# A two-layer graph attention kernel: moving layer 1's softmaxes, its selection matrices and its key gathers

## The chip, the cores and the metric

The kernel runs on one core of a Trainium2 chip. The metric is the device time of one execution in microseconds. Before the change three runs took 2463.49, 2476.31 and 2496.46 us; the median, 2476.31 us, is the time to be compared.

## The reference

A graph of N = 3125 nodes with 768 features has 53125 edges (both directions of 25000, and one loop per node), sorted by destination, each of one of three relations. Two layers of relational graph attention follow each other, and a layer norm of the residual ends it. One layer is

```
xr = einsum('nd,rdf->rnf', x, W)            # every node, every relation
oi, oj = xr[etype, dst], xr[etype, src]
alpha = leaky_relu(oi @ q + oj @ k, 0.2)    # per edge and head
e = exp(alpha - segment_max(alpha, dst)[dst])
a = e / (segment_sum(e, dst)[dst] + 1e-16)
out = segment_sum(a * oj, dst) + b
```

with four heads of 192 features in layer 1 and one head of 768 in layer 2. Between the layers stands an elu; the result is `layernorm(x + layer2(elu(layer1(x))))`. All values are float32.

## The kernel before

The nodes are cut into NB = 25 blocks of 128 destinations. The edges of a block are held in slots of 128 edges: SL = 18 slots a block, SLL = 9 in the last and smaller one, NK = 441 in all. An edge is a partition, a slot a column.

Matrix products of nearly float32 accuracy are made of reduced-precision parts: an operand is split in a high part H and a remainder L, and three products (H·H, H·L, L·H) are summed. Where one operand is exact, as a 0/1 matrix is, two are enough.

The work has four stages, each emitted in an order written out by hand; each engine runs its own instructions in that order:

- **Preparation** (`prepare`, `weights_kq`, `nodes_kq`): edge lists are put into DRAM, and the weights are split into `wH` and `wL`, kept in SBUF. Each node's key and query values are computed for every relation: the keys go to the DRAM table `kt1`, the queries stay in SBUF and are split in three bf16 parts, `q1s`.
- **Layer 1's products and softmaxes** (`phase1`): 144 groups of 18 matmuls make `xr`, half a row (384 columns) of one block and relation each (`d_group`, L629). ScalarE copies a group from PSUM into one of three row buffers (`d_row`, L641), and every second group sends the row to the DRAM table `tab1` on SP's queue. Between the groups stand the steps of the softmaxes, one block for each six groups: `a_index` and `a_index2` turn the edge lists into gather indices `ridx` and local destinations `dl`; `a_gathers` fetches the keys of 18 slots from `kt1` with indirect DMAs that GpSimd issues (L451); `a_q`, `a_q2`, `a_q3` bring the queries to the edges; `a_alpha` (L565) adds keys and queries; `a_max` (three TensorE transposes, L573), `a_scan` (two VectorE scans, and ScalarE's Exp, L586), `a_back` (a transpose) and `a_put` give the weights `pall`. The list `steps` holds at which group each step of a block stands: its gathers five groups before the block's first group, `a_alpha` four after, `a_max` five after; block 24 has a list of its own, `last`. Three buffers `kt0` to `kt2` hold the keys. Layer 2's weights are split in the same stage, and x plus a bias is stored for the end (`w_load`, `w_split`, `d_split`).
- **Layer 1's sums and layer 2's products** (`phase2`): a loop over slots k. GpSimd gathers the 128 rows of slot k from `tab1` into one of the nine buffers `share` (L451). `high` makes H, the rows times the edge weights, on ScalarE, four instructions (L788), and `sel`, a 128 x 128 matrix that is 1 where an edge (partition) belongs to a destination (column), with one compare on VectorE for each third slot, on GpSimd for the others (L790). `low` makes the remainder L on VectorE (L802), and `sums` multiplies `sel` with H and L into PSUM, four matmuls (L821). Slot k is gathered in step k, reaches `high` in step k+5, `low` in k+6 and `sums` in k+8 (LAG = 8). A few of the first eight slots take another form (`whole`). When a block is complete, `e_y` to `e_s2` give the elu and its transposes (L833 to L864), and 108 matmuls (`d_part`, L876), six for each slot of the next block, make layer 2's rows for the table `tab2`. The blocks come in the order 24, 0, 1, ... 23.
- **Layer 2's sums** (`phase3`): the same for one head, with the softmaxes inside the loop, and the layer norm.

All work of `phase2` on `tab1` begins when its last row has been stored, since any edge may need any row.

Of the kernel before, what the change touches and what calls it, by code (L numbers as in the profile page):

```python
# [45 lines left out]
PART = 6  # L46

# [4 lines left out]
def kernel(  # L52
# [50 lines left out]
    w2_d = dram.tile([R * DT * P, 2 * D], F32, name="w2_d")  # L103

# [16 lines left out]
    q1s = keep.tile([P, NB, H1, R, 3], BF, name="q1s")  # L121
# [344 lines left out]

    def a_load(pre, b):
        s = a_st[b] = {}
        r0 = start(b, regs)
        s["T"] = pre.tile([3 * SL, P], F32, name="T", bufs=2)  # L470
        nc.sync.dma_start(s["T"], at(ed_d, 0, 0, [[LL, 3], [P, SL], [1, P]], r0))
# [26 lines left out]
    def phase1(pre, work, psum, wH, wL, qq):  # L498
        kts = [work.tile([P, SL, H1], F32, name=f"kt{i}", bufs=1) for i in range(3)]
# [3 lines left out]
        rows = share[:3]  # L503
# [4 lines left out]
        def a_window(b):  # L508
            s = st[b]
            s["f"] = work.tile([H1 * SL, 3 * P + 1], F32, name="w", bufs=2)  # L510
            nc.sync.dma_start(s["f"], at(ed_d, 3, -P - 1, [[P, SL], [0, H1], [1, 3 * P + 1]], start(b, regs)))
# [15 lines left out]

        def a_gather(b, j):
            gather_rows(kts[b % 3][:, j, :], kt1, b, j)
# [19 lines left out]
        def a_q3(b):  # L549
# [9 lines left out]
            s["qe"] = work.tile([P, SL, H1], F32, name="qe", bufs=2)  # L559
            V.tensor_reduce(s["qe"], tq, AX.X, ALU.add)  # L560

        def a_alpha(b):
            s = st[b]
            a = work.tile([P, SL, H1], F32, name="a", bufs=2)
            V.tensor_add(a, s["qe"], kts[b % 3])  # L565
            s["al"] = als[b % 2]
            V.scalar_tensor_tensor(s["al"][:, 1:SL + 1, :], a, NEG_SLOPE, a, op0=ALU.mult, op1=ALU.max)

        def a_max(b):
            s = st[b]  # L570
            pa = psum.tile([P, 512], F32, name="pa", bufs=1)
            for c in range(3):
                T.transpose(pa[:H1 * SL, c * P:(c + 1) * P],  # L573
                            s["al"].rearrange("p j h -> p (j h)")[:, c * H1:(c + SL) * H1], ident)
            s["pa"] = pa

        def a_scan(b):
            s = st[b]
            pa, f = s["pa"], s["f"]
            F, B = (share[i][:H1 * SL, b % 2 * HW:b % 2 * HW + n] for i, n in ((7, 3 * P), (8, 2 * P)))  # L580
            V.tensor_tensor_scan(F, f[:, 0:3 * P], pa[:H1 * SL, :3 * P], -3e38, op0=ALU.add, op1=ALU.max)
            V.tensor_tensor_scan(B[:, ::-1], f[:, P + 1:3 * P + 1][:, ::-1], F[:, P:3 * P][:, ::-1], -3e38,
                                 op0=ALU.add, op1=ALU.max)
            s["e"] = work.tile([H1 * SL, P], F32, name="e", bufs=2)
            V.tensor_sub(s["e"], pa[:H1 * SL, P:2 * P], B[:, :P])
            S.activation(s["e"], s["e"], AF.Exp)  # L586

        def a_back(b):
            s = st[b]
            pT = s["pT"] = psum.tile([P, 512], F32, name="pT", bufs=1)  # L590
            T.transpose(pT[:, :H1 * SL], s["e"], ident[:H1 * SL, :H1 * SL])

        def a_put(b):
            pT = st.pop(b)["pT"]
            V.tensor_copy(pall[:, b].rearrange("p j h -> p (j h)"), pT[:, :H1 * SL])
# [39 lines left out]
        def d_row(b, r, c):  # L635
# [3 lines left out]
            o = rows[len(n_rows) % 3]  # L639
# [28 lines left out]
        def slots(b):  # L668
            return SLL if b == NB - 1 else SL

        a_index(0)
        a_index2(0)
        for j in range(SL):
            a_gather(0, j)
        for b in range(2):
# [6 lines left out]

        def a_gathers(b):
            for j in range(slots(b)):
                a_gather(b, j)
# [7 lines left out]
        def x_next(b):  # L693
# [6 lines left out]
        ev = {}  # L700

        steps = ((-9, a_loads), (-9, a_loads2), (-6, a_index), (-5, a_index2), (-5, a_gathers), (1, a_q), (2, a_q2),
                 (2, a_window), (3, a_q3), (4, a_alpha), (5, a_max), (6, a_scan), (7, a_back), (8, a_put))
        last = ((-14, a_loads), (-9, a_loads2), (-9, a_index), (-8, a_index2), (-8, a_gathers), (-4, a_q), (-3, a_q2),
                (-3, a_window), (-2, a_q3), (-1, a_alpha), (0, a_max), (1, a_scan), (2, a_back), (3, a_put))
        for b in [*reversed(range(NB - 1)), NB - 1]:
            for d, f in steps if b < NB - 1 else last:

                d += 2 * (d >= 4 and b < 8)
                if 6 * b + d >= 0:  # L710
                    ev.setdefault(6 * b + d, []).append((f, b))
# [3 lines left out]
        for n in range(max(ev) + 1):  # L715
# [25 lines left out]
            if 0 < n <= len(groups):  # L741
                d_row(*groups[n - 1])


    def phase2(work, psum, wH, wL):
# [10 lines left out]
        blk = {}  # L756

        order = [NB - 1, *range(NB - 1)]
        ends2 = {SLL + i * SL - 1 for i in range(NB)}

        def slot(k):

            if k < SLL:
                return NB - 1, k
            return divmod(k - SLL, SL)
# [9 lines left out]
        def high(k):  # L775
# [13 lines left out]
            sel = work.tile([P, P], F32R, name="sel", bufs=4)  # L789
            (V if k % 3 == 0 else G).tensor_scalar(sel, row, dl[:, b, j:j + 1], None, op0=ALU.is_equal)  # L790
            st[k] = [sel, H]

        def low(k):
# [4 lines left out]
            H = st[k][1]  # L798
# [7 lines left out]
        def sums(k):  # L806
# [11 lines left out]
            sel, H, L = st.pop(k)  # L818
            for i, a in enumerate((H, L)):
                for c in range(2):  # L820
                    T.matmul(acc[:, c, :HW], sel, a[:, c * HW:(c + 1) * HW], start=(j == 0 and i == 0),  # L821
# [78 lines left out]

        LAG = 8
        first = SLL + LAG - 1
# [842 lines left out]
```

## Time and profile before

| | |
|---|---|
| median of the timed runs | 2476.31 us |
| the profiled execution's own time | 2296.29 us |
| its span | 2294.5 us |
| mean granted TensorE clock | 0.955 |
| TensorE, VectorE, ScalarE, GpSimd busy | 2047.2, 1685.4, 1172.9, 1749.5 us |
| first gather of keys | 123.2 us |
| first gather of `tab1`'s rows | 738.2 us |
| first and last elu (L839) | 763.3 and 1581.0 us |
| moved by DMA | 508.20 MB |

The profile was taken in one execution. TensorE is PE (PEld loads its stationary operand), VectorE DVE, ScalarE ACT, GpSimd POOL; SP is the engine that issues most plain DMAs. Matmuls are pipelined, so that one that follows another shows some 340 ns and costs 177. A wait is named by who waited and what ended it last. "issue" is time in which the engine waited for nothing that the profile shows. The profiled execution is shorter than any of the timed ones; the two are kept apart below.

### The profile page before, as it was taken

How to read it: one execution, taken by the hardware profiler on the slowest of the kernel's cores; microseconds unless marked ns; L12 is line 12 of the kernel's file. 1: busy time of each engine (PE TensorE's matmuls, PEld its weight loads, DVE VectorE, ACT ScalarE, POOL GpSimd, SP SyncE). 2: the span in 40 equal slices, each digit the busy share in tenths (PEclk: the TensorE clock that was granted, in tenths of full speed). 3: DMA queues.
4: the chain of work that ended last, by engine and by line, in shares of the span. 5: the costliest groups of instructions: out<-in, count | busy, mean ns of one | idle time of the engine just before them, and what ended most of it. 6: DMA issues, size and time to landing. Idle time of an engine off the chain costs nothing.

```text
span 2294.5 us, 37251 instructions
## 1 busy us (share of the span) xinstructions
PE 2047.2 (89%) x11055; PEld 1758.8 (77%) x11055; DVE 1685.4 (73%) x4377; ACT 1172.9 (51%) x2620; POOL 1749.5 (76%) x1685
## 2 busy tenths in 40 slices
PE   6998878998885899999999999999498898899886
PEld 5888878888885889999999999999255555555554
DVE  7734434434432899999999999995388888898887
ACT  5411111111111788888888888884144444444443
POOL 4267777777776888888888888883777777777773
PEclk9999999999998899999999999999699999999998
DMA  6554544444455977778777777775888888888882
GB/s 178 179 154 158 177 137 158 165 153 143 158 191 166 316 237 232 228 231 244 236 229 234 230 234 238 232 231 202 282 280 293 288 296 279 286 278 283 282 269 72
DMA packets 153593, 508.20 MB, mean 221 GB/s; under 512 B 40404, under 2 KB 53723, under 8 KB 153383
## 3 DMA queue, kind: packets, MB, share of 16 engines
q0 software_dynamic: 85472, 334.19, 48.1%
q1 hardware_dynamic: 57681, 155.56, 18.8%
q10 hardware_dynamic: 10230, 15.98, 2.2%
q8 instruction: 91, 1.49, 0.3%
q14 instruction: 119, 0.97, 0.1%
HBM read 428.40 MB, written 94.04 MB: 228 GB/s over the span
## 4 chain that ended last, share of the span: by engine, by line
PE 35%; DVE 14%; POOL 7%; issue 6%; DMA 5%; ACT 1%; POOLq 0%; DVEq 0%; ACTq 0%
PE po L876 15%; PE acc L821 11%; PE acc L1091 7%; DMA G<-ftab,ridx 4%; DVE L L1080 4%; POOL share L451 3%; POOL sel L790 2%; DVE selp L1062 1%; DVE L L802 1%; DVE sT L986 1%; POOL G L451 1%; DVE sel L1071 1%; DMA G<-ftab,rfirst 1%; PE pt L851 1%; DVE stats L1109 1%
## 5 line engine op out<-in xcount | busy, mean ns | idle before, releaser
L788 ACT ACTIVATE H<-share,pall 128x193 fp32r<-128x193 f32 x1748 | 644.0, 447 | 106.9 <-DMA share<-ftab,ridx 43.5
L802 DVE SCALAR_TENSOR_TENSOR L<-share,pall,H 128x193 fp32r<-128x193 f32 x1748 | 648.9, 437 | 28.6 <-ACT H L788 14.1
L876 PE MATMUL po<-wH,hT 128*128 128x386 f32 (+1 forms) x1800 | 533.2, 339 | 0.0
L451 POOL DMA_INDIRECT G<-ftab,ridx x378 | 432.5, 1144 | 115.2 <-issue 54.0
L451 POOL DMA_INDIRECT kt<-kt,ridx x378 | 405.7, 1073 | 115.2 <-issue 114.6
L451 POOL DMA_INDIRECT share<-ftab,ridx x378 | 428.6, 1134 | 81.4 <-DVE L L802 42.6
L629 PE MATMUL po<-wH,xT 128*128 128x384 f32 x1584 | 445.2, 354 | 0.4 <-issue 0.2
L1091 PE MATMUL acc<-G,selp 128*128 128x386 f32 x904 | 355.5, 519 | 1.1 <-DVE selp L1062 1.1
L876 PEld LDWEIGHTS po<-wH,hT 128*128 128x128 f32 x1800 | 334.6, 189 | 0.6 <-DVE hT L864 0.5
L876 PE MATMUL po<-wL,hT 128*128 128x386 f32 (+1 forms) x900 | 304.9, 339 | 0.0
L629 PEld LDWEIGHTS po<-wH,xT 128*128 128x128 f32 x1584 | 302.1, 196 | 2.9 <-DVE xT L616 0.5
L629 PE MATMUL po<-wL,xT 128*128 128x384 f32 x792 | 275.4, 348 | 0.0
L821 PE MATMUL acc<-H,sel 128*128 128x386 f32 x874 | 241.9, 358 | 22.0 <-POOL sel L790 12.1
L641 ACT COPY share<-po 128x384 f32<-128x384 f32 x144 | 69.0, 479 | 339.4 <-PE po L629 274.4
L1091 PEld LDWEIGHTS acc<-G,selp 128*128 128x128 f32 x904 | 169.7, 199 | 89.1 <-issue 23.0
L790 POOL TENSOR_SCALAR sel<-frow,fdl 128x128 fp32r<-128x128 f32 x291 | 224.8, 773 | 13.4 <-PE acc L821 1.5
L821 PE MATMUL acc<-L,sel 128*128 128x386 f32 x874 | 226.5, 340 | 0.0
L1080 DVE SCALAR_TENSOR_TENSOR L<-G,p,H 128x772 fp32r<-128x772 f32 x215 | 217.5, 1013 | 1.4 <-issue 0.7
L1066 ACT ACTIVATE H<-G,p 128x772 fp32r<-128x772 f32 x215 | 189.8, 927 | 47.5 <-issue 34.0
L821 PEld LDWEIGHTS acc<-H,sel 128*128 128x128 f32 x874 | 149.8, 189 | 55.7 <-POOL sel L790 46.7
L565 DVE TENSOR_TENSOR a<-qe,kt 128x72 f32<-128x72 f32 x25 | 5.9, 238 | 242.3 <-DMA kt<-kt,ridx 205.3
L876 PEld LDWEIGHTS po<-wL,hT 128*128 128x128 f32 x900 | 169.7, 189 | 0.0
(229 smaller groups left out, 2902.8 us busy)
## 6 DMA issues: line engine op xcount, KB each, us to landing
ftab<-r SPq DMA_DIRECT2D x75, 386.0 KB
ftab<-share SPq DMA_DIRECT2D x72, 386.0 KB
sT<-dr_d SPq DMA_DIRECT2D x25, 576.0 KB
share<-in_L_gnn_W_dram SPq DMA_DIRECT2D x36, 384.0 KB
w_d<-w2hl SPq DMA_DIRECT2D x18, 768.0 KB
share<-in_x_dram SPq DMA_DIRECT2D x25, 384.0 KB
xb_d<-share SPq DMA_DIRECT2D x25, 384.0 KB
xr<-in_x_dram SPq DMA_DIRECT2D x23, 384.0 KB
```

The source lines that it names most:

```text
L451: G.indirect_dma_start(out=to, out_offset=None, in_=tab, in_offset=_index(i[:, j:j + 1]), bounds_check=NP * R - 1, oob_is_err=False)
L629: T.matmul(po[:, :HALF], xT[:, s, t, :], w[:, i, sl], start=(n == 0), stop=(n == 3 * DT - 1))
L641: S.copy(to, po[:, :HALF].rearrange("p (h f) -> p h f", h=2))
L788: S.activation(H[:, c], g[:, c], AF.Copy, scale=pall[:, b, j, h:h + 1])
L790: (V if k % 3 == 0 else G).tensor_scalar(sel, row, dl[:, b, j:j + 1], None, op0=ALU.is_equal)
L802: V.scalar_tensor_tensor(L[:, c], g[:, c], pall[:, b, j, h:h + 1], H[:, c].bitcast(F32), op0=ALU.mult, op1=ALU.subtract)
L821: T.matmul(acc[:, c, :HW], sel, a[:, c * HW:(c + 1) * HW], start=(j == 0 and i == 0), stop=(k in ends2 and i == 1), skip_group_check=True)
L851: T.transpose(pt[:, t // 3, (t % 3) * P:(t % 3 + 1) * P], s["ey"][:, t * P:(t + 1) * P], ident)
L876: T.matmul(po[:, :wd], hT[:, k, t, :], w[:, r * DT + t, sl], start=(t == 0 and n == 0), stop=(t == DT - 1 and n == 2))
L1066: S.activation(H, g, AF.Copy, scale=p)
L1080: V.scalar_tensor_tensor(L, g, blk[b]["p"][:, j:j + 1], st[k][1].bitcast(F32), op0=ALU.mult, op1=ALU.subtract)
L1091: T.matmul(acc[:, c, :HW], sel, a[:, c * HW:(c + 1) * HW], start=(j == 0 and i == 0), stop=(k in ends and i == len(parts) - 1))
```

## The change

- **The order and pace of the softmaxes.** `phase1` takes the blocks in the order of `phase2`: 24, 0, 1, ... 23. With i a block's place in it, gathers stand at group 6i-5, the queries at 7i+3 or earlier (at least five groups before those of the next block, and within the 144 groups), and `a_alpha` to `a_put` at 7i+6 to 7i+10, so one block for each seven groups.
- **The last five blocks** (SPILL = 5) get their queries in `phase1`, kept in `qlast`, which lies in the memory of `q1s` where that is no longer needed. Their softmaxes run in `phase2`'s loop (`c_window` to `c_put`), in the gap after a block's elu, with `y` and `ey` as scratch. For the last three (LATE = 3) the 54 key gathers are issued there too, one every five slots.
- **The keys** are gathered straight into `pall`, where the weights come later; `kt0` to `kt2` are gone. GpSimd clears `pall` at the start.
- **The selections** are made in `phase1` by ScalarE: Abs(dl - row) for each slot, and for six slots at once Relu(1 - that), in the buffer `share[6]`; SP stores the six in the new DRAM table `sel_d` (74 stores). In `phase2` SP loads them back, two slots at a time, into three buffers (221 loads), a load being asked for when `sums` has used a pair.
- **A fourth row buffer** in `phase1`.

The steps `a_alpha` to `a_put` keep their instructions; they are taken out of `phase1` so that both stages can use them.

```diff
+    G.memset(pall, 0.0)
...
+    def a_gather(b, j):
+        gather_rows(pall[:, b, j, :], kt1, b, j)
...
+        rows = [*share[:3], work.tile([P, RW], F32, name="row3", bufs=1)]
...
+            i = order1.index(b) - (NB - SPILL)
+            s["qe"] = qlast[i] if i >= 0 else work.tile([P, SL, H1], F32, name="qe", bufs=5)
...
+        def s_slot(k):
+            b, j = slot1(k)
+            S.activation(share[6][:, k % SC * P:(k % SC + 1) * P], row, AF.Abs, bias=dl[:, b, j:j + 1], scale=-1.0)
+        def s_store(c):
+            n = (min((c + 1) * SC, NK) - c * SC) * P
+            to = share[6][:, :n]
+            S.activation(to, to, AF.Relu, bias=1.0, scale=-1.0)
+            nc.sync.dma_start(sel_d[c * P:(c + 1) * P, :n], to)
...
-        for b in [*reversed(range(NB - 1)), NB - 1]:
-            for d, f in steps if b < NB - 1 else last:
+        for i, b in enumerate(order1):
+            when = []
+            q = min(7 * i + 3, NG - 1 - 5 * (NB - 1 - i))
+            if i > 1:
+                when += [(6 * i - 14, a_loads), (q - 8, a_loads2)]
+            if i > 0:
+                when += [(6 * i - 6, a_index), (6 * i - 5, a_index2)]
+                if i < NB - LATE:
+                    when += [(6 * i - 5, a_gathers)]
+            when += [(q, a_q), (q + 1, a_q2), (q + 2, a_q3)]
+            if i < NB - SPILL:
+                when += [(7 * i + d, f) for d, f in ((2, b_window), (6, b_alpha), (7, b_max), (8, b_scan), (9, b_back),
+                                                     (10, b_put))]
...
+        for k in range(NK):
+            i = order1.index(slot1(k)[0])
+            n = max(6 * i - 4, k // 3)
+            ev2.setdefault(n, []).append((s_slot, k))
+            if k % SC == SC - 1 or k == NK - 1:
+                ev2.setdefault(n, []).append((s_store, k // SC))
...
+        def s_load(c):
+            k = 2 * c
+            if k >= NK:
+                return
+            n = min(2, NK - k) * P
+            sels[c] = work.tile([P, 2, P], F32R, name="sel", bufs=3)
+            nc.sync.dma_start(sels[c].bitcast(F32).rearrange("p s n -> p (s n)")[:, :n],
+                              sel_d[k // SC * P:(k // SC + 1) * P, k % SC * P:k % SC * P + n])
...
-            sel = work.tile([P, P], F32R, name="sel", bufs=4)
-            (V if k % 3 == 0 else G).tensor_scalar(sel, row, dl[:, b, j:j + 1], None, op0=ALU.is_equal)
...
-                    T.matmul(acc[:, c, :HW], sel, a[:, c * HW:(c + 1) * HW], start=(j == 0 and i == 0),
+                    T.matmul(acc[:, c, :HW], sels[k // 2][:, k % 2], a[:, c * HW:(c + 1) * HW], start=(j == 0 and i == 0),
...
+        late = [(b, j) for b in order[NB - LATE:] for j in range(SL)]
+        for i, (b, j) in enumerate(late):
+            when(20 + 5 * i, a_gather, b, j)
+        for i, b in enumerate(order[NB - SPILL:]):
+            k = 20 + 5 * SL * max(i + 1 - (SPILL - LATE), 0) + 4
+            m = max(k - SLL - LAG, 0) // SL + 1 + (i if i < SPILL - LATE else 0)
+            k = SLL + m * SL + LAG + 6
+            for d, f in ((0, c_window), (4, c_alpha), (4, c_max), (5, c_scan), (6, c_back), (7, c_put)):
+                when(k + d, f, b)
...
             if 0 <= k - LAG < NK:
                 sums(k - LAG)
+                if (k - LAG) % 2:
+                    s_load((k - LAG) // 2 + 3)
```

## The prediction

> **What bounds the kernel now.** I read the page's slices first, then busy time by stage, then the waits of each stage, then the tiles on its critical wait.
>
> ```profile
> PE   6998878998885899999999999999498898899886
> ...
> POOL 4267777777776888888888888883777777777773
> PEclk9999999999998899999999999999699999999998
> ```
>
> Each digit is a 57 us slice. Three stages stand out, cut at the two dips. Busy time in each (engines in the order PE, PEld, DVE, ACT, POOL, then clock, DMA share, GB/s):
>
> ```profile
> 122.00:737.00 615.00, 532.51 (x3303) 510.63 (x3303) 241.49 (x521) 107.13 (x210) 471.55 (x441) 0.95 0.49 161
> ...
> 763.00:1581.00 818.00, 802.04 (x4430) 767.52 (x4431) 781.67 (x2272) 709.12 (x1911) 705.38 (x713) 1.00 0.77 236
> ...
> 1607.00:2294.00 687.00, 577.95 (x2439) 354.92 (x2439) 555.26 (x1273) 279.29 (x335) 514.43 (x453) 0.92 0.81 266
> ```
>
> The first is layer 1's products with its softmaxes (phase1), the second layer 1's sums with layer 2's products (phase2), the third layer 2's sums. In the first, TensorE is idle for 82 us and its clock is below full. The key gathers, from the tile's view, and the waits of the stage (in total, times, longest) say why:
>
> ```profile
> L451 POOL DMA_INDIRECT kt<-kt,ridx x378: 992/997/1769, 196.5 to 716.1; - x189
> L451 POOL DMA_INDIRECT kt<-kt,rfirst x63: 992/997/1582, 123.2 to 727.8; - x63
> ```
>
> ```profile
> DVE a L565 <- DMA kt<-kt,ridx: 205.3, 21, 15.1
> ...
> POOL kt L451 <- issue: 133.1, 437, 0.3
> PEld pa L573 <- DVE al L567: 73.0, 22, 9.0
> PE pa L573 <- DVE al L567: 66.1, 22, 8.7
> ```
>
> 441 gathers start from 123.2 to 727.8 us: 604.6/440 = 1.374 us each (997 ns and 0.30 of "issue"), with no other gap. GpSimd paces the stage; VectorE waits for the keys, and TensorE, in order, for VectorE at the transposes `pa`. One such stop, and the end of the stage:
>
> ```profile
> 420.53 0.86 PE L573 MATMUL pa<-fident,al 128*72 128x128 f32 x3 [2.42 <-DVE al L567]
> ...
> 421.83 0.84 PE L629 MATMUL po<-wH,xT 128*128 128x384 f32 x2
> ```
>
> ```profile
> 738.24 1.00 POOL L451 DMA_INDIRECT share<-ftab,rfirst  x1 [9.42 <-ACT e L586]
> ```
>
> After the 2.42 us stop a pair of matmuls takes 0.84 us where it took 0.52. At the end GpSimd idles 9.4 us while the last softmax and table row finish.
>
> In the second stage the waits name GpSimd again, but they are small:
>
> ```profile
> PEld acc L821 <- POOL sel L790: 46.7, 106, 2.4
> ```
>
> ```profile
> L790 POOL TENSOR_SCALAR sel<-frow,fdl 128x128 fp32r<-128x128 f32 x291 | 224.8, 773 | 13.4 <-PE acc L821 1.5
> ...
> L790 DVE TENSOR_SCALAR sel<-frow,fdl 128x128 fp32r<-128x128 f32 x146 | 45.8, 314 | 0.0
> ```
>
> GpSimd's 705 busy and 0.3 us of issue for some 430 gathers fill its 818 us; VectorE is at 96% and TensorE at 98%. Three engines are within a few per cent of the bound.
>
> **What the Trainium skill says.** "TensorE: Matmul & The Clock Gate", Part 1: after about an idle window of 3.4 us the array runs at half clock until it has been busy as long again. The trace agrees: 0.84 against 0.52 us above. So a wait removed here gives back more than itself. "GPSIMD Engine Reference", Specifications: its SBUF interface is shared with VectorE, with contention where a VectorE instruction has two SBUF inputs. L802 has two, and its durations run from 400 (median 409) to 687 ns, which fits but does not prove it. "ScalarE: Activation LUTs", Table sets: abs and relu are in every set, so Abs, Relu, Exp and Copy should need no table load; no run here shows it. "DMA: Bandwidth & Descriptors", Anatomy of one DMA: about 2 us fixed and little for 128 KB; the chain of waits has a 386 KB table store landing in 2.33 us.
>
> **The change part by part.**
>
> *Key gathers, first stage.* 54 of 441 (last three blocks) leave it. 387 x 1.374 = 532 us, from 123.2 to 655. The destination `pall` needs no buffer to come free; a block's gathers wait only for its index, made 6i-5 groups in, always earlier than GpSimd arrives.
>
> TensorE without stops: between two stops in the timeline 18 matmuls take 3.18 us, six groups with the transposes 21.2. 144 groups are 24 x 21.2 = 509 us, from 122 to about 631. (Check: 532 busy, less about 25 at half clock.) Softmax i now sits at group 7i+6, at 122+3+3.53(7i+6) = 146+24.7i; its last key is issued at 134+24.7i and is used 3.7 us later (727.83 to 731.56 in the timeline). Some 8 us to spare for every i: the stops go. GpSimd at 655 is then later than TensorE and its last table row (631 + 0.5 copy + 2.3 landing). Sums start at about 658 instead of 738.2: **-80 us**. The 9.4 us tail is in it.
>
> *Selections.* ScalarE gets 441 Abs of 128 columns with a pointer bias. The Trainium skill's price ("ScalarE: Activation LUTs", What ACT_TABLE_LOAD costs) is 280 + 0.833 x 128 = 387 ns, less 93 of overlap; L586, 72x128, took 310. I take 0.31: 137 us. Plus 74 Relu of 768 columns at 0.83 (as the cast L660): 61. ScalarE goes from 107 to 305 of 530 us. One staging tile, `share[6]`, must be stored before the next six are made: about 2.6 us, covered by the 3.5 us of a product group before ScalarE is due there again. Without that cover: 74 times the excess. The stores stand on SP ahead of table rows and loads. On GpSimd 225 us go, on VectorE 46.
>
> *Their loads.* 221 of 128 KB on SP, three buffers, each asked for when TensorE has done with a pair and needed four slots later: 5 x 1.77 - 0.7 = 8 us. At 2.3 to 5 us landing they cost nothing; above 8, everything behind them on TensorE stands.
>
> *Second stage.* Blocks pass at (1581.0-763.3)/24 = 34.07 us (first and last start of L839). Ten matmuls of a slot take 1.77 us undisturbed, six transposes 0.57: 18 x 1.77 + 0.57 = 32.4. At most 24 x 1.65 = 40 us. VectorE: 782 - 46 + 14 = 750 of 790, still under TensorE; GpSimd: 432 x 1.4 + 54 x 1.374 = 680, no longer full.
>
> *Five late softmaxes there.* Each: one window load, VectorE 0.24+0.23+0.94+0.69+0.29+0.22 = 2.6 us, one exp of 0.31, four transposes, some 0.7 us of TensorE. In front of c_max TensorE waits for c_alpha, which is queued behind a slot's L; sums and products are queued behind that. Bounds: nothing to 4 us each (the longest waits for `ey`, same pattern, are 4.5); I take 1.5 with the transposes: +7. The rest of the sums' waits (H from gathers, end of stage) I leave in for +9. **-24 us**.
>
> *Fourth row buffer, order of blocks, clearing `pall`.* No wait for rows is in the waits; GpSimd is idle for 60% of the first 122 us. Nothing, from -3 to +3.
>
> Sum: the profiled execution was 2296.3 us (span 2294.5 and 1.8 around it): 2296 - 80 - 24 = 2192. The timed runs, median 2476.31, are 180 us above it, and the profile can't show where. I carry the gain over as it is: **2372 us** (in proportion: 2364).
>
> **The rivals.**
> *A, ScalarE's staging.* If each store holds ScalarE 1.1 us beyond cover (SP in order, behind a load that waits for VectorE), products end 81 us later, at 712, and sums start at 717: gain 21+24, 2431 us. For it: one buffer, 74 round trips, two product banks only. Against it: ScalarE idle 500 of 615 us, DMA share 0.49.
> *B, the DMA engines: slower.* The second stage moves 236 GB/s x 818 us = 193 MB; the selections add 441 x 64 KB = 29 MB. My 786 us need 282 GB/s. If today's 236 is all that random rows and 1 KB packets allow, the stage takes 941 us: +123 - 80 = +43, 2519 us. It decides below 222 MB/(818+80 us) = 247 GB/s. Against it: layer 2's sums run at 280 to 293 GB/s with the same kind of gathers, at a DMA share of 0.86.
> *C, more than forecast.* All 40 us of the second stage and proportional runs: (80+38)/2296 of 2476, 2349, and with cheaper VectorE from a quiet GpSimd down to 2330.
> *The change is not what it says* only if keys still gate TensorE; the 8 us of slack speaks against it.
>
> **Chances.** Forecast 0.58 (2345 to 2410), A 0.17 (2410 to 2460), C 0.12, B 0.13 (2480 to 2565; the upper end is 225 GB/s). Range 2322 to 2455: it leaves out B, the end of A and the end of C, 2 in 10. Two per cent, about what a measurement here can tell from no change, is 2427 and 2526: faster 0.73 (forecast, C, a sixth of A), within 0.19 (the rest of A and some of B), slower 0.08 (the rest of B).
>
> **What would show it.** Key gathers every 1.374 us up to about 655; no `pa` wait on VectorE above 1 us; clock 1.00 in the first stage; first gather of `share` near 658; L839's analogue every 32.5 us; ScalarE some 300 us in the first stage. I am wrong if ScalarE's Abs waits for the store and TensorE for its bank, if sums wait for `sel` loads, or if H waits for gathers at 280 GB/s.

## The result, and the profile after

The changed kernel takes 2537.27 us (median of four runs, 2534.68 to 2540.57). The kernel before takes 2486.39 us (four runs, 2463.49 to 2497.07). The ratio is 1.027, with a 95% interval of 1.022 to 1.032: the change makes the kernel slower, where 2372 us had been forecast. Ratios and their intervals are taken over the fast runs alone and so differ a little from the quotient of the medians. The profiled execution took 2535.16 us, with a span of 2533.3 and a mean TensorE clock of 0.910.

One thing has to be said before the two profiles are compared: the profiled execution of before (2296 us) does not come from the conditions of its timed runs (2463 to 2497 us). In what follows the kernel before takes 2294 and 2303 us on two chips and 2479, 2510 and 2521 us in three series on two others. I call them chips of the first kind and of the second kind. By its time the profile of before is one of the first kind, that of after one of the second. No chip was met in both kinds, so whether the difference lies in the chip itself or in what surrounded it at the time is not shown.

The slices of the page, of the kernel after (one digit is 63 us here):

```profile
PE   6968788778878778989899999999758989898887
...
POOL 4266646655662066777677676767267777777773
PEclk9978788898988889999899999999879989998899
```

TensorE is at 7 or 8 tenths in the first stage and GpSimd no longer at 7, but at 4 to 6, and lower still once its gathers are done. No engine is full there. The three stages by busy time (PE, PEld, DVE, ACT, POOL, then clock, DMA share, GB/s), cut as before:

```profile
122.00:886.00 764.00, 604.78 (x3284) 552.92 (x3284) 230.29 (x502) 297.24 (x723) 413.04 (x392) 0.85 0.50 168
912.00:1790.00 878.00, 817.04 (x4454) 790.91 (x4453) 710.11 (x2150) 703.99 (x1907) 616.77 (x478) 0.97 0.78 251
1816.00:2533.00 717.00, 585.13 (x2439) 357.55 (x2439) 555.17 (x1273) 280.07 (x335) 509.54 (x453) 0.90 0.77 255
```

The first stage has 764 us instead of 615, the second 878 instead of 818, and the third, whose code is as it was, 717 instead of 687. GpSimd's busy time fell as forecast (413 us in the first stage, 617 in the second), and so did VectorE's (782 to 710). ScalarE got its 190 us more. The work moved; the time didn't follow. The waits of the first stage (in total, times, longest):

```profile
ACT share L688 <- remote: 168.1, 31, 20.2
POOL pall L461 <- DVE rel L575: 136.7, 17, 12.7
ACT share L636 <- DMA sel_d<-share: 114.0, 48, 7.5
...
PEld po L676 <- issue: 105.0, 121, 4.0
...
PE po L676 <- issue: 77.1, 100, 3.7
```

In the profile of before GpSimd waited for nothing but its own issue. Here it waits 136.7 us for the index that VectorE makes (`a_index2`), so it is held up, not holding up. ScalarE waits 114 us for the staging tile's stores (L636, Abs), which the forecast held to be covered. And TensorE's weight loads stop 121 times on "issue": nothing that the profile can name. "remote" on ScalarE is a wait whose end the profile can put to no instruction and no DMA.

Both words need care in these traces. Of the semaphore signals that the engines' instructions send, the traces of the second kind hold 60 to 85%, stage by stage, those of the first kind 99 to 100%. So a wait for another engine can show as "issue" or "remote" there. In the second stage VectorE has such stops, nearly all before instructions that do wait for a semaphore:

```profile
DVE L L867 <- issue: 112.4, 74, 5.8
```

### The profile page after: what moved, and what is told of

Same layout as the page of the kernel before. It is cut to its first block, busy times and chain, and to the rows that moved or that the text cites. A ratio compares the mean times of both kernels' runs of the same rounds, so it can differ in the third digit from the quotient of the medians.

```text
span 2533.3 us, 37524 instructions
## 1 busy us (share of the span) xinstructions
PE 2138.6 (84%) x11055; PEld 1825.0 (72%) x11055; DVE 1604.0 (63%) x4233; ACT 1360.5 (54%) x3135; POOL 1595.6 (63%) x1395
## 4 chain that ended last, share of the span: by engine, by line
PE 31%; DVE 13%; issue 5%; DMA 3%; POOL 2%; another core or an unknown queue 1%; ACT 1%; POOLq 0%; DVEq 0%; ACTq 0%
PE po L941 12%; PE acc L1193 9%; PE acc L886 8%; DVE L L867 3%; DVE L L1182 3%; DMA G<-ftab,ridx 2%; POOL G L461 1%; DVE selp L1164 1%; ACT H L855 1%; DVE sT L1088 1%; DVE sel L1173 1%; PE pt L916 1%; PE bc L1082 1%; DVE stats L1211 1%
## 5 line engine op out<-in xcount | busy, mean ns | idle before, releaser
L867 DVE SCALAR_TENSOR_TENSOR L<-share,pall,H 128x193 fp32r<-128x193 f32 x1748 | 601.8, 413 | 144.2 <-issue 112.4
L461 POOL DMA_INDIRECT share<-ftab,ridx x378 | 501.2, 1326 | 199.7 <-DVE L L867 77.1
L461 POOL DMA_INDIRECT pall<-kt,ridx x378 | 406.4, 1075 | 236.6 <-DVE rel L575 115.0
L676 PE MATMUL po<-wH,xT 128*128 128x384 f32 x1584 | 476.9, 373 | 68.2 <-issue 50.5
L676 PEld LDWEIGHTS po<-wH,xT 128*128 128x128 f32 x1584 | 324.3, 210 | 91.3 <-issue 69.9
L676 PE MATMUL po<-wL,xT 128*128 128x384 f32 x792 | 291.7, 368 | 21.6 <-issue 21.1
L636 ACT ACTIVATE share<-frow,fdl 128x128 f32<-128x128 f32 x441 | 145.1, 394 | 121.6 <-DMA sel_d<-share 114.0
L886 PEld LDWEIGHTS acc<-L,sel 128*128 128x128 f32 x874 | 164.7, 194 | 33.7 <-DVE L L867 19.6
L676 PEld LDWEIGHTS po<-wL,xT 128*128 128x128 f32 x792 | 166.7, 211 | 28.4 <-issue 27.7
L688 ACT COPY share<-po 128x384 f32<-128x384 f32 x108 | 51.3, 475 | 247.6 <-remote 168.1
```

The costliest lines, as they stand in the source:

```text
L461: G.indirect_dma_start(out=to, out_offset=None, in_=tab, in_offset=_index(i[:, j:j + 1]), bounds_check=NP * R - 1, oob_is_err=False)
L636: S.activation(share[6][:, k % SC * P:(k % SC + 1) * P], row, AF.Abs, bias=dl[:, b, j:j + 1], scale=-1.0)
L676: T.matmul(po[:, :HALF], xT[:, s, t, :], w[:, i, sl], start=(n == 0), stop=(n == 3 * DT - 1))
L688: S.copy(to, po[:, :HALF].rearrange("p (h f) -> p h f", h=2))
L867: V.scalar_tensor_tensor(L[:, c], g[:, c], pall[:, b, j, h:h + 1], H[:, c].bitcast(F32), op0=ALU.mult, op1=ALU.subtract)
L886: T.matmul(acc[:, c, :HW], sels[k // 2][:, k % 2], a[:, c * HW:(c + 1) * HW], start=(j == 0 and i == 0), stop=(k in ends2 and i == 1), ski ...
```

## The experiments

The expectations name their theories by letters; each says what it stands for. Where stages are compared, I take them from the tile view of `H`, whose first and last start bound the stage of sums: the first stage runs from 122 us to the first `H`, the second from there to the last, and "rest" is what is left of the span.

### Each part alone, on a chip of the first kind

The kernel before as it is, in one more execution:

> The kernel before, unchanged, with a new profile. The first profile (2296 us) is some 190 us below every timed run (2463 to 2497), and the changed kernel's profile shows TensorE pausing about 0.7 us between matmuls with nothing waited for. Theory S (the pauses belong to the chip's state in these runs, not to the change): about 2480 us, with such pauses in the first stage and key gathers that no longer run back to back. Theory K (the pauses come with the changed kernel): about 2300 us, no pauses.

2289.89 us, span 2288.1, clock 0.956. This is theory K's number; its cause falls below, where the kernel before has the pauses too.

The gathers alone: the changed kernel, with the selections compared by VectorE and GpSimd as before.

```diff
-        for c in range(3):
-            s_load(c)
...
-            st[k] = [H]
+            sel = work.tile([P, P], F32R, name="sel", bufs=4)
+            (V if k % 3 == 0 else G).tensor_scalar(sel, row, dl[:, b, j:j + 1], None, op0=ALU.is_equal)
+            st[k] = [sel, H]
```

> The changed kernel with the selections made where they were before (VectorE and GpSimd compares in the second stage); no Abs, no Relu, no selection stores or loads. Theory T (making and storing the selections is what costs): faster than before, 2400 to 2450 us. Theory P (the new pace of the softmaxes costs): slower than before, 2530 us or more.

The selections alone: the kernel before with Abs and Relu on ScalarE, the one staging tile, `sel_d` and its loads.

```diff
+        def s_slot(k):
+            b, j = slot1(k)
+            S.activation(share[6][:, k % SC * P:(k % SC + 1) * P], row, AF.Abs, bias=dl[:, b, j:j + 1], scale=-1.0)
...
-            (V if k % 3 == 0 else G).tensor_scalar(sel, row, dl[:, b, j:j + 1], None, op0=ALU.is_equal)
```

> The kernel before with the selections through DRAM alone: softmaxes, key buffers and the three row buffers as before, the eight first-block selections made last. Theory T: slower than before, 2550 us or more. Theory P: same or faster, 2430 to 2490 us.

The whole change with two staging tiles; the room for the second comes from the fourth row buffer.

```diff
-        rows = [*share[:3], work.tile([P, RW], F32, name="row3", bufs=1)]
+        rows = share[:3]
...
+            stage = [share[6], work.tile([P, SC * P], F32, name="stage", bufs=1)]
...
-            to = share[6][:, :n]
+            to = stage[c % 2][:, :n]
```

> The changed kernel with two staging buffers for the selections in place of one, and three row buffers in place of four. Theory T1 (ScalarE's wait for the store of its one staging buffer, 114 us in the profile, holds TensorE): 2440 to 2490 us. Theory T2 (the stores and loads cost as DMA traffic, whoever waits): 2530 us, as the change itself.

Measured, with the kernel before at 2293.57 us (median of 17 runs):

| | us | ratio (95%) | first stage to | second | rest |
|---|---|---|---|---|---|
| before | 2293.57 | | 744 | 825 | 719 |
| gathers alone | 2288.65 | 0.997 (0.995 to 0.999) | 666 | 900 | 720 |
| selections alone | 2265.26 | 0.987 (0.983 to 0.991) | 746 | 804 | 717 |
| both, two staging tiles | 2192.93 | 0.955 (0.952 to 0.959) | 664 | 813 | 721 |

Here the forecast's mechanism is seen, part by part. The gathers bring the first stage down by 79 us (80 forecast). Alone they are worth nothing, because the second stage, with gathers and compares on GpSimd, grows by 75. The wait for GpSimd's compares in the gathers' variant:

```profile
PEld acc L882 <- POOL sel L851: 111.9, 140, 2.1
...
PE acc L882 <- POOL sel L851: 68.6, 70, 1.8
```

Only the selections make that room. Alone the two parts bring 5 and 28 us, together 101, where 104 had been summed. The stages of the profiles add up to 90 of it, since the profiled execution is the slowest of its four runs. The one staging tile is not covered even here. ScalarE's wait in the selections' variant is 2.9 us at each of 68 stores:

```profile
ACT share L606 <- DMA sel_d<-share: 200.1, 68, 10.5
```

It cost nothing in that kernel, because GpSimd set the pace of the stage. With two tiles no such wait is left. No theory of a part that is bad by itself (T or P) was borne out here, and the pauses of S and K don't show either: they need the other kind of chip.

### The change and its staging, on a chip of the second kind

The changed kernel as it is:

> The changed kernel as it is, beside the kernel before and three variants of it, on one chip. Theory Q (the single staging tile costs the gain: ScalarE waits for each of the 74 stores before it may write the next Abs, and the evictions behind it hold up the products): the first stage takes 30 to 80 us more than the 543 us that the variant with two staging tiles took, the ScalarE waits for stores come to 150 to 250 us, and the time is 2225 to 2280 where the kernel before takes 2294. Theory C (the condition of the chip in the first comparison made both kernels slow and the change lost its gain to it): on a chip where the kernel before takes 2294, this one takes 2190 to 2205, the staging costs nothing, and only where the kernel before takes about 2490 it is slower.

With three row buffers and one staging tile:

```diff
-        rows = [*share[:3], work.tile([P, RW], F32, name="row3", bufs=1)]
+        rows = share[:3]
...
-            o = rows[len(n_rows) % 4]
+            o = rows[len(n_rows) % 3]
```

> The changed kernel with three row buffers instead of four, the staging as changed (one tile). Theory Q: the fourth row buffer does not matter, so the same as the changed kernel within 10 us. Against it, if the fourth buffer is what hides or brings the staging wait: more than 20 us apart from the changed kernel. Theory C: the same as the changed kernel and as the variant with two staging tiles.

With the staging tile in two halves:

```diff
-            n = (min((c + 1) * SC, NK) - c * SC) * P
-            to = share[6][:, :n]
+            w = SC // 2
+            n = (min((c + 1) * w, NK) - c * w) * P
+            at = c % 2 * w * P
+            to = share[6][:, at:at + n]
```

> The changed kernel with its one staging tile used as two halves of three selections each: 147 Relus and 147 stores of 192 KB, each half written while the other is stored; four row buffers. Theory Q: the wait shrinks from about 2.9 us at each of 74 stores to under 1 us, so most of the loss is won back: within 15 us of the variant with two staging tiles, though with 73 more Relus of about 0.5 us on ScalarE. If the wait is for the whole tile all the same, it grows with 147 stores instead and the time is above the changed kernel's. Theory C: no gain over the changed kernel.

With two staging tiles, as above:

> The changed kernel with two staging tiles and three row buffers, once more, on the chip of the three others. Theory Q: about 0.955 of the kernel before, and 30 to 80 us less than the changed kernel. Theory C: the same as the changed kernel; on a chip where the kernel before takes about 2490, above it like the changed kernel.

The kernel before takes 2509.72 us here (20 runs). The change takes 2570.41 (1.024; 1.015 to 1.034), with three row buffers 2568.04 (1.019; 1.010 to 1.028), with halves 2552.85 (1.015; 1.012 to 1.018), with two tiles 2547.82 (1.015; 1.009 to 1.022). The fourth row buffer is worth nothing, as forecast. Staging is worth some 20 us of the median; in this series' profiles the first `H` moves from 920 to 874 us. (The change's other two profiles have it at 886 and 911, so a single profile gives the size only roughly.) So theory Q is right that the single tile costs, but its 0.955 did not come: the same kernel that gains 4.5% on the first kind of chip still loses 1.5% here, as theory C had it for such a chip. The staging isn't the main loss.

### Each part alone, on a chip of the second kind

> The kernel before as it is, for its trace beside the three others. Two chips have been met: one on which it takes 2294 us at a granted clock of 0.955, one on which it takes 2510 at 0.916. Theory H (on the second chip TensorE is handed its instructions in stretches at one per 0.70 us; the kernel before hides part of that in the idle time of its first stage, the changed one has no such idle time): there its first stage ends at 800 to 860 instead of 744, with 60 to 120 us of such stretches in the first stage, most of them not on the path; the second stage takes 880 to 900 instead of 836. Theory G (the pauses come from the change's own traffic): its first stage shows fewer than a third of the changed kernel's pauses. On the first chip: as the record of it, a first stage that ends at 744 and four to six stretches of 2 to 5 us.

> The changed kernel as it is. On the chip on which the kernel before takes about 2294: theory Q (the single staging tile costs 30 to 80 us) 2225 to 2280, with 150 to 250 us of ScalarE's waiting for the stores; against it, if the staging is hidden, 2190 to 2205. On the chip on which the kernel before takes about 2510: 2555 to 2585, as before.

> The changed kernel with its selections compared by VectorE and GpSimd as in the kernel before (no staging, no stores and loads of selections), the key gathers as changed. On the slower chip, theory H: the first stage loses its cover here too, so it is no faster than the kernel before there, 0.995 to 1.02; its first stage ends as late as the changed kernel's, 870 to 910. Theory G (the selections' traffic through DRAM brings the pauses): first stage ends at 740 to 800 and it is 2 to 4 per cent faster than the kernel before. On the faster chip: 0.997 as measured.

> The kernel before with its selections computed by ScalarE and sent through DRAM, the key gathers as before. On the slower chip, theory H: the first stage ends about where the kernel before's does and the second is shorter, 0.98 to 1.0. Theory G: the first stage ends 60 us or more later than the kernel before's on the same chip, 1.02 to 1.04. On the faster chip: 0.987 as measured.

Before takes 2520.52 us here (23 runs). The change takes 2572.01 (1.023; 1.014 to 1.032), the gathers alone 2532.01 (1.005; 1.003 to 1.008), the selections alone 2554.41 (1.014; 1.005 to 1.023). The stages of these profiles, and of the two-tile variant from the series above:

| | first stage to | second | rest |
|---|---|---|---|
| before | 906 | 841 | 756 |
| gathers alone | 870 | 899 | 763 |
| selections alone | 967 | 836 | 758 |
| the change | 911 | 899 | 756 |
| both, two staging tiles | 874 | 901 | 761 |

For the kernel before theories H and G both miss: H has its first stage end at 800 to 860, G has few pauses in it. It ends at 906, as late as the change. For the gathers alone H's numbers came (870, and 1.005). For the selections alone G's 60 us in the first stage came (967 against 906), its 1.02 to 1.04 did not. The change itself lies in its 2555 to 2585. The view of `H`, of the kernel before, here and on the first kind of chip:

```profile
L788 ACT ACTIVATE H<-share,pall x1748: 437/443/474, 905.7 to 1746.9; 128x193 fp32r<-128x193 f32 x195
```

```profile
L788 ACT ACTIVATE H<-share,pall x1748: 436/443/480, 744.4 to 1568.9; 128x193 fp32r<-128x193 f32 x195
```

So 161 of the 215 us between the two executions lie in the first stage. The waits of the kernel before in that stage, on the second kind of chip:

```profile
ACT share L641 <- remote: 291.8, 32, 35.7
DVE xT L616 <- ACT xT L615: 217.7, 19, 31.3
POOL kt L451 <- DVE rel L526: 146.8, 22, 13.3
PEld po L629 <- issue: 127.3, 94, 15.9
...
PE po L629 <- issue: 109.7, 78, 14.9
```

The same picture as in the change: the stops come with the second kind of chip, not with the change. On the first kind TensorE has no stop of this sort in this stage. GpSimd's 441 gathers, 604.6 us from first to last in the profile of the forecast, take 741.9 us here, as they wait for VectorE's index. A stage that GpSimd doesn't pace gains little from fewer gathers: 36 us instead of 79.

What the stops look like, in the timeline of the kernel before (start, duration, engine, line, operation, idle time before it and what ended it):

```profile
350.56 0.34 PE L629 MATMUL po<-wH,xT 128*128 128x384 f32 x1
...
351.52 0.48 ACT L641 COPY share<-po 128x384 f32<-128x384 f32 x1 [7.00 <-PE po L629]
...
353.54 0.50 PE L629 MATMUL po<-wH,xT 128*128 128x384 f32 x2
...
355.76 0.30 PEld L629 LDWEIGHTS po<-wH,xT 128*128 128x128 f32 x2 [0.89 <-issue]
...
356.05 1.00 POOL L451 DMA_INDIRECT kt<-kt,ridx  x1 [0.30 <-issue]
...
357.19 0.19 PEld L629 LDWEIGHTS po<-wH,xT 128*128 128x128 f32 x1 [0.95 <-issue]
...
357.36 1.00 POOL L451 DMA_INDIRECT kt<-kt,ridx  x1 [0.30 <-issue]
358.66 1.00 POOL L451 DMA_INDIRECT kt<-kt,ridx  x1 [0.30 <-issue]
359.96 1.00 POOL L451 DMA_INDIRECT kt<-kt,ridx  x1 [0.31 <-issue]
360.82 0.48 ACT L641 COPY share<-po 128x384 f32<-128x384 f32 x1 [8.81 <-issue]
...
361.35 0.69 PE L629 MATMUL po<-wH,xT 128*128 128x384 f32 x1 [3.72 <-issue]
```

A product group ends at 350.90 us. ScalarE is free from 352.00, but copies it at 360.82 only. TensorE meanwhile falters in the middle of the next group, which ends at 357.6, and then stands for 3.72 us: the group after it needs the bank that this copy frees, since there are two. So the mark "issue" has two meanings here. In the whole stage TensorE has 132 us of such stops of over 0.35 us; 42 of them stand before matmuls that wait for no semaphore, the others before ones that do.

The copies measure the stops without the signals on record. There are 144 groups and 144 copies, in the same order. Counted from where the group has ended and ScalarE is free, the copies of the kernel before start late by 10 us in all on the first kind of chip (0.39 at most), and by 333 us on the second, 44 of them by over 1 us.

All this goes on while GpSimd issues one gather after another and the DMA engines are nearly idle (4 GB/s from 352 to 360 us). I sorted the first stage of this trace by how many gathers in a row, each within 0.45 us of the last, GpSimd had issued up to then. At the first seven of a row (248 us of the stage) TensorE's stops come to 3 us, from the eighth on (361 us) to 115, outside rows (173 us) to 14. On the first kind of chip 590 us from the twelfth gather of a row on bring none. In the second stage of the kernel before GpSimd has a compare between its gathers, no row is longer than four, and TensorE has no such stop.

Two rivals can be read from the same traces. If the instructions came late from memory, their DMA packets should differ: there are 47 of them in this stage on either kind, and the longest takes 1.8 us on the second and 1.9 on the first. If the gathers piled up in the DMA engines, their packets should start late: the first of a gather starts 1.73 us after its issue in the median on the second kind, 1.87 on the first.

### The rows broken up

To the variant with two staging tiles I added small fills on GpSimd after every fourth gather of the first two stages: one, five or twelve. They have no effect on the output.

```diff
+    brk = keep.tile([P, 64], F32, name="brk")
+    calls = [0]
...
+        if tab is not tab2:
+            calls[0] += 1
+            if calls[0] % 4 == 0:
+                for _ in range(5):
+                    G.memset(brk, 0.0)
```

> The variant with two staging tiles and three row buffers, and after every fourth indirect gather of the first two stages one small fill of 64 columns on GpSimd (an addition without effect on the result). In the traces of the slower chip TensorE's pauses in the first stage lie almost only where GpSimd has issued eight or more indirect gathers without a break. Theory R1 (it is the unbroken row of gathers that counts): a short fill ends the row, TensorE's pauses in the first stage fall from about 105 us to under 30, the first stage ends at 740 to 800 instead of 874, and the time is 2400 to 2470 where the kernel before takes about 2510. Theory R2 (it is the rate of gathers, one per 1.30 us, that counts): a fill of some 0.1 us changes little, 2530 to 2560. Theory N (the rows of gathers only mark the place where the other engines are stopped by something else): no change, 2530 to 2560. On the faster chip: no pauses to remove, 2195 to 2225.

> The same with five such fills after every fourth gather, about 1 us of work in all. Theory R1 and R2: on the slower chip TensorE's pauses in the first stage fall under 30 us, the first stage ends at 740 to 800, the time is 2400 to 2480. Theory N: the pauses stay at 90 to 120 us and GpSimd's added 100 us or so are hidden or come on top, 2540 to 2620. On the faster chip the first stage is paced by GpSimd, which gets about 100 us more: 2270 to 2310.

> The same with twelve such fills after every fourth gather, some 2 us or more. Theory R1 and R2: no pauses, the first stage paced by GpSimd's own work, ending at 780 to 860. If only this one shows few pauses, the rate counts, and its bound lies between the two. Theory N: pauses as without it. On the faster chip 2380 to 2450.

The chip was one of the second kind; the kernel before takes 2478.95 us on it (23 runs).

| fills | us | ratio (95%) | first stage to | second | TensorE's stops, first stage |
|---|---|---|---|---|---|
| none (another chip of this kind) | 2547.82 | 1.015 (1.009 to 1.022) | 874 | 901 | 112 us, 129 times |
| one | 2504.87 | 1.013 (1.010 to 1.017) | 853 | 900 | 102 us, 140 times |
| five | 2447.94 | 0.987 (0.975 to 0.999) | 788 | 921 | 13.5 us, 5 times |
| twelve | 2740.25 | 1.106 (1.093 to 1.120) | 926 | 1070 | 0.8 us, twice |

TensorE's longest waits on "issue" in the first stage, with one fill:

```profile
PE po L685 <- issue: 86.8, 119, 3.1
```

and all of them with five:

```profile
PE pa L508 <- issue: 12.8, 3, 6.0
PE pT L572 <- issue: 0.7, 2, 0.3
```

The timeline of GpSimd tells why one fill does nothing. With one:

```profile
308.06 1.00 POOL L463 DMA_INDIRECT pall<-kt,ridx  x1 [0.30 <-issue]
309.05 0.17 POOL L469 MEMSET brk<- 128x64 f32 x1
309.38 1.00 POOL L463 DMA_INDIRECT pall<-kt,ridx  x1 [0.16 <-issue]
```

and with five:

```profile
301.94 1.00 POOL L463 DMA_INDIRECT pall<-kt,ridx  x1 [0.30 <-issue]
302.94 1.01 POOL L469 MEMSET brk<- 128x64 f32 x5
304.52 1.00 POOL L463 DMA_INDIRECT pall<-kt,ridx  x1 [0.57 <-issue]
```

One fill hides in the 0.30 us between two gathers: they still start 1.32 us apart. Five put them 2.58 us apart, one gather in four, so that the mean goes from 1.30 to 1.62 us. So an instruction between gathers is not enough (R1 as it was put falls), and theory N falls too: stops that something else brings would not go when GpSimd's gathers are parted. Giving GpSimd more to do in a stage made that stage shorter by 64 us against one fill, on the same chip. ScalarE's late copies, counted as above, go from 224 us with one fill to 14 with five and 8 with twelve. Twelve fills had been expected to end the stage at 780 to 860; they cost more than that.

In the first stage the five fills lower the mean pace and also end the rows at four, so that stage can't tell R2's rate from the length of a row. The second stage can. VectorE's stops ahead of its `L`, with one fill and with five:

```profile
DVE L L876 <- issue: 117.0, 68, 5.7
```

```profile
DVE L L876 <- issue: 16.5, 34, 2.3
```

The mean pace there is nearly the same, one gather per 1.84 and per 1.87 us. But with one fill 354 of 491 gathers stand in rows of eight or more, with five none do. That speaks for the long row at full rate, against the mean pace. Not all of it is gained, since VectorE's waits for `H` rise from 30 to 68 us, and in this stage the fills cost more than they saved: 921 us instead of 900.

### The same fills where there are no stops

The fills, five after every fourth key gather, in the kernel before; in the kernel before with the selections and a staging tile in halves; and in the two-tile variant, in the first stage alone.

```diff
+        if tab is kt1:
+            calls[0] += 1
+            if calls[0] % 4 == 0:
+                for _ in range(5):
+                    G.memset(brk, 0.0)
```

> The kernel before with five small fills on GpSimd (about 0.8 us of work, an addition without effect) after every fourth key gather, nothing else. On a chip where the kernel before takes 2450 to 2530, theory R2 (indirect gathers at one per 1.30 us stop the other engines there; at one per 1.5 us they don't): TensorE's pauses in the first stage fall from about 130 us to under 30, the first stage ends at 800 to 850 instead of 906 although GpSimd has about 110 us more to do, and the kernel is 2 to 4 per cent faster than without the fills. Against it, if the pauses of the kernel before have another cause: the first stage ends later by up to 110 us. On a chip where the kernel before takes 2294, its first stage is paced by GpSimd: 2380 to 2410.

> The kernel before with its selections by ScalarE through DRAM (staging tile in two halves), no late softmaxes, and the fills after every fourth key gather in the first stage. On a slower chip by R2: first stage ends at 800 to 850, second stage 836 us as in the variant with the selections alone, 2390 to 2440 where the kernel before takes about 2490. On a chip where the kernel before takes 2294: 2360 to 2400.

> The variant with two staging tiles, three late softmax gathers and the fills after every fourth key gather only, none behind the row gathers of the second stage. On a slower chip by R2: the first stage as with fills everywhere (sums from about 790), the second stage 880 to 900 instead of 921 if the fills cost more there than the pauses do, so 2420 to 2445 where the fills everywhere gave 2448; if the pauses of the second stage matter more, 2450 to 2480. On a chip where the kernel before takes 2294: 2260 to 2290.

The chip was one of the first kind: the kernel before takes 2302.71 us (7 runs). The three take 2447.96 (1.064; 1.062 to 1.067), 2404.61 (1.045; 1.043 to 1.048) and 2335.41 us (1.015; 1.013 to 1.017). They were slower than expected by 38, 5 and 45 us, since the fills cost more than I had put them at. The view of `H` of the kernel before with fills:

```profile
L795 ACT ACTIVATE H<-share,pall x1748: 437/444/473, 892.1 to 1720.7; 128x193 fp32r<-128x193 f32 x195
```

and of the two-tile variant with fills in the first stage, here and, with fills in both stages, on the chip of the second kind:

```profile
L864 ACT ACTIVATE H<-share,pall x1748: 438/444/478, 784.6 to 1614.5; 128x193 fp32r<-128x193 f32 x195
```

```profile
L864 ACT ACTIVATE H<-share,pall x1748: 438/443/472, 788.1 to 1709.0; 128x193 fp32r<-128x193 f32 x195
```

Two things follow. Where there are no stops GpSimd paces the first stage of the kernel before, as the forecast had it: 110 breaks put the first `H` 148 us later than the 744 on the other chip of this kind, 1.34 us each. And with the rows ended at four the first stage takes until 785 us on the first kind of chip and 788 on the second: the second kind has no handicap left in this stage, where it had 210 us (664 against 874) with long rows.

No run has the kernel before with fills on a chip of the second kind; that its first stage would gain from them is not shown.

## Why the prediction was wrong

**The total.** The step that failed is "The timed runs, median 2476.31, are 180 us above it, and the profile can't show where. I carry the gain over as it is". Such a difference is not an even tax: of the 215 us between two executions of before, three quarters lie in the first stage, the one that the largest term came from, and they change what bounds it. Against the execution that it was summed from, the sum held: 2192 us, and the two-tile variant takes 2192.93 on a chip of that kind. That it fits to a microsecond is luck: the first stage gave its 80 us, the second half of its 24. The changed kernel itself, with its one staging tile, was not run on such a chip.

**Key gathers, -80 us.** "GpSimd paces the stage" is right for the profile shown, measured at -79. On the second kind of chip it is wrong: GpSimd waits 147 us for VectorE there, and the same edit gives -36 (906 to 870). Stops also cost clock: it is 0.85 in the first stage of the profile after, and 0.97 in that of the two-tile variant on the first kind. The stop of 2.42 us in the prediction's lines was enough for a stretch at half clock (420.48 to 423.89 us), though it is shorter than the window that is cited there.

**Selections, "covered by the 3.5 us of a product group".** Not covered. The waits are 2.4 us at 48 stores in the profile after, and 2.9 at 68 on the first kind of chip. In the first stage they cost 46 us on the second kind (920 against 874), in the median 23. This is rival A's mechanism at about half of its 81 us. The selections alone move the end of the first stage there from 906 to 967. Abs was priced at 0.31 us and takes 145.1 us for 441, 0.33 each, with 0.394 in the mean for a single one. That agrees with the 387 ns, and the overlap of one with the next, 97 ns in the median, with the 93, that the prediction took from the Trainium skill ("ScalarE: Activation LUTs", What ACT_TABLE_LOAD costs). Abs come in threes, so one in three has none to overlap with. No table load came with Abs and Relu: there are 46 before and 46 after.

**Their loads, nothing.** Nearly right: TensorE waits once for 17 us at the start of the stage, in the profile after, and hardly at all later.

**Second stage, -24 us.** On the first kind of chip -12: the elu goes from one per 33.91 to one per 33.46 us, not 32.4. On the second kind +58 (841 to 899). VectorE, named in the forecast only as busy to 96%, waits 112 us ahead of its `L`, and the trace doesn't say for what. What fits is that the compares taken off GpSimd had been the breaks between its gathers. From the first kind of chip to the second this stage grows by 16 us in the kernel before and not at all with the gathers alone, neither of which has rows of eight gathers or more; by 32 with the selections alone, where 207 of 438 gathers stand in such rows; and by 88 with both and two tiles, where 290 of 492 do. The gathers alone and both parts together have the same mean pace there, one per 1.83 us. But no run made this stage shorter by breaking the rows, so it stays argued. The gathers' variant takes its 899 us on both kinds, by GpSimd's compares. One part was left out of the forecast and only named in rival C: VectorE's `L` takes 413 ns in the mean after and 437 before.

**Rival B** (DMA engines) is out on the first kind of chip: the two-tile variant moves 281 GB/s in this stage, 282 had been needed. **The fourth row buffer** is nothing, as said.

What stays open is how a long row of gathers stops the other engines, and why on some chips alone. The profile shows no queue and no packet for it. Every run on record comes with a span and a clock, so whether recording has a part in the stops is open too. The third stage, with other gathers, is 37 to 43 us longer on the second kind with the same kernel; whether for the same cause was not tried.

## What to carry to other kernels

When the profiled execution and the timed runs of one kernel are 7% apart, find out first in which stage the difference lies: a bound read from one need not hold in the other. Stops that end on "issue" or "remote" on several engines at once, while one engine goes on, are worth sorting by what that engine does; and before such a mark is believed, look whether the trace holds the signals. And an engine made faster can cost others time. With stops of this kind, breaking up the rows of indirect gathers was worth some 2% against one fill and about 1% against the kernel before, the latter barely clear of noise (0.975 to 0.999); on chips without them the same fills are a loss.

## What was not expected of the hardware

- The same kernel takes 2294 us on one chip and 2510 on another, 9% apart, and two kernels change places: two staging tiles are 0.955 of before on the one, 1.015 on the other.
- On the slower chips long rows of GpSimd's indirect gathers, one per 1.30 us, go with stops of TensorE, VectorE and ScalarE; hardly any of TensorE's fall on the first seven of a row. With a pause of 1.28 us more after every fourth, TensorE's fell from 102 us to 13.5 in the first stage, and that stage ended 64 us earlier although GpSimd had more to do.
- The traces of the slower chips lack 15 to 40% of the engines' semaphore signals, those of the faster ones next to none.
- No version was shown to beat the kernel before on both kinds of chip: with five fills it takes 2447.94 against 2478.95 us on the second (0.987, its interval up to 0.999), without fills 2192.93 against 2293.57 on the first.
